# A GRU with a routed FFN on one core: norms of dispatched tokens from SBUF by products with ones, and the chunk work two steps sooner

## The chip, the core and the metric

The kernel runs as one program on one NeuronCore of a Trainium2 chip. The core has five engines that run their own instruction queues in order and meet by semaphores: TensorE (PE, matmuls; PEld is its weight load), VectorE (DVE), ScalarE (ACT), GpSimd (POOL) and SyncE (SP, which here only issues DMAs). The metric is the device time of one execution in microseconds (us); lower is better.

## The reference

A GRU runs over 256 time steps for 16 sequences of width 512. Its outputs are the tokens of a mixture of 8 low-rank experts, and the result is added to x:

```python
def cell(h, x):
    gi = x @ W_ih + b_ih
    gh = h @ W_hh + b_hh
    r = sigmoid(i_r + h_r); z = sigmoid(i_z + h_z)
    n = tanh(i_n + r * h_n)
    h_new = (1 - z) * n + z * h
# for every token h of the 16 x 256:
norm = maximum(linalg.norm(h), 1e-12)
routing = softmax(h / norm @ router_w)          # 8 experts
rw, experts = top_k(routing, 2); rw /= sum(rw)
out = x + sum over the two experts of rw[e] * (h @ Wa[e] @ Wb[e])   # Wa 512x128, Wb 128x512
```

All is float32. Each step of the GRU needs the one before, so the steps form a recurrence; the FFN of finished tokens can run beside it.

## The kernel before

**The recurrence.** `step` issues one GRU step. The state h lies transposed in `hist` (128 partitions: 4 groups of 32 columns; free: 8 steps of a block x 4 quarters q x 48). PE multiplies it with W_hh into PSUM banks `rn` (r and the hidden part of n, L914) and `z` (L924). ACT takes tanh for r (L940), z (L945) and n (L949), DVE does the arithmetic in between (n: L947, L948; zh: L952; m: L954; rows: L956) and transposes the new state back into `hist` (L959). The next step's first matmul waits for that transpose. `back` (L967) makes a row form of h. The input gates x W_ih (`gate_in`, L281 and L289) are done for two steps at a time, half in each step, behind z; for 12 pairs (`EARLY`) they are computed long before and only copied in (`seed`, L261, on ACT).

**Blocks, chunks, slabs.** 8 steps of 16 sequences make a block of 128 tokens. Of 32 blocks the first 29 are *dispatched* and the last 3 are *dense* (`Moe`: all 8 experts). The dispatched blocks form 4 chunks of 7, 11, 7 and 4 blocks (`CHUNKS`). For each block a `Route` keeps its rows in HBM (`keep`: 8 DMAs to H), computes the router's logits (`logits`, L353), the norm, a softmax (`soft1`) and the top two (`soft2`). When a chunk is complete, `Chunk` ranks its tokens by expert (`ranks`, `places`), loads the rows from H again (`fetch`, L545) and scatters them into slots in HBM sorted by expert, by two indirect DMAs per block on POOL (L551). Then each `Slab` (128 slots, one expert) is loaded (L652), gets its expert's weights by two POOL copies (L670, L674), is transposed on DVE (L680), goes through two pairs of PE pieces (`down` L691, `up` L706) with ACT copies between (L698, L714), and is stored to HBM. `Combine` gathers each token's two results by indirect DMAs on POOL (L743), adds them with their weights to x on DVE (L757) and stores the output.

**What sets the order.** All these are agents with a list of `Piece`s. In each step `choose` picks pieces whose gap (steps since the agent's last piece) has passed and whose rooms (buffers) are free. Routes and chunks go first; slabs have a due time `by`, and their rate is the work left over the steps left. `advance(0, ...)` issues the pieces' PE work behind the step's gates, `advance(1, ...)` their other work behind `back`. The order so made is then fixed on every engine. `LAG` sets when slabs start: `ready` is a chunk's end + LAG + its blocks. After step 256 the loop goes on with what is left: the end of the slabs, the combines and the dense blocks.

**The Route of a block before.** Steps from the block's end: +1 `keep`; +2 `logits`, then `fetch` (L605: SP reloads the block's 128 rows from H into `ht`) and `soft0` (DVE transposes the logits, L615); +4 `norm` (L620: ACT squares `ht` with a sum along the row; L622: POOL takes the root); +5 `soft1`; +6 `soft2`. The chunk's `ranks` come 7 steps behind the chunk's end. The dense blocks do without a reload: POOL squares h from SBUF (`prep`, L780 and L785), and 16 products with a column of ones (L796) put the sums beside the logits in `rt`.

Of the kernel before, what the change touches and what calls it, by code (L numbers as in the profile page):

```python
# [8 lines left out]
FP = mybir.dt.float32  # L9
# [7 lines left out]
AF = mybir.ActivationFunctionType  # L17
ALU = mybir.AluOpType
# [3 lines left out]
P = 128  # L22
TS = 8
CHUNKS = [7, 11, 7, 4]
LAG = 10

EARLY = list(range(82, 128, 4))

# [16 lines left out]
def gru_moe_kernel(  # L45
# [47 lines left out]
    pe, dve, act, pool, sp = nc.tensor, nc.vector, nc.scalar, nc.gpsimd, nc.sync  # L93
    B, T, D = x.shape
    E, _, R = wa.shape
    NJ = D // P
    NQ = P // 32
# [18 lines left out]
    moe = ctx.enter_context(tc.tile_pool(name="moe", bufs=2))  # L116
# [29 lines left out]
    for side, src in enumerate((b_ih, b_hh)):  # L146
        for g in (0, 2, 1):
            tag = ("xg", "wbg")[side]
# [34 lines left out]
    ones = const.tile([P, 1], FP, name="ones")  # L183
    pool.memset(ones, 1.0)
    half = const.tile([P, 1], FP, name="half")
# [37 lines left out]
    rt = ps_r.tile([P, 512], FP, name="rt")  # L223
    pe.matmul(rt, lhsT=zero[:, 0:P], rhs=zero, start=True, stop=True)
    banks = []
    for n in range(2):
        pair = []
        for what in ("rn", "z"):
            g = ps_g.tile([P, 512], FP, name=f"{what}_{n}")
            for j in range(NJ):  # L230
                pe.matmul(
                    g[32 * j : 32 * j + 32, :], lhsT=zero[:, 0:32], rhs=zero,
                    start=True, stop=True,
# [5 lines left out]
    for n, parts in enumerate((((0, 0), (1, 0)), ((1, 2),), ((0, 2),), ((0, 1), (1, 1)))):  # L239
        for k, (side, g) in enumerate(parts):  # L240
            for j in range(NJ):
                pe.matmul(
                    bias_ps[32 * j : 32 * j + 32, n * P : (n + 1) * P],
                    lhsT=ones_sq[0:1, 0:32],
                    rhs=b_rows[side, g][:, j * P : (j + 1) * P],
                    start=(k == 0), stop=(k == len(parts) - 1),
# [97 lines left out]
    def tokens(h, q, c):  # L344

        b0 = 16 + 4 * c
        return h[:, :, q, b0 : b0 + 4].rearrange("p t b -> p b t")

    def router(h):

        for q in range(NQ):
            for c in range(NJ):
                pe.matmul(  # L353
                    rt[32 * c : 32 * c + E, 0:32].rearrange("p (b t) -> p b t", t=TS),
                    lhsT=wr_sb[:, q, :], rhs=tokens(h, q, c),
                    start=(q == 0), stop=(q == NQ - 1),
                )

    class Early:
# [55 lines left out]
        def plan(self):  # L415
            pieces = [
                Piece(then=[("load",)], takes="early"),
                Piece(gap=2, then=[("turn",)], takes="at"),
            ] + [
                Piece(gap=0, cost=c, pe=[("into", what, q)])  # L420
                for what, c in (("rn", 0.43), ("z", 0.22))
                for q in range(NQ)
            ] + [Piece(then=[("store",)], gives="early")]
            pieces[2].gap, pieces[2].takes = 1, ["ps"]
            pieces[9].then, pieces[9].gives = [("keep",)], ["ps", "at"]
            return pieces


    class Chunk:
# [113 lines left out]
        def fetch(self, k):  # L543
            ht = moe.tile([P, D], FP, tag="ht2", bufs=2, name=f"ht2_{self.c}_{k}")
            sp.dma_start(ht, self.rows[k].rearrange("b t d -> (b t) d"))  # L545
            self.ht = getattr(self, "ht", {})
            self.ht[k] = ht
# [21 lines left out]
        def plan(self):  # L569
            k = self.k  # L570
            pieces = [
                Piece(gap=7, cost=0.9, pe=[("ranks",)],
                      then=[("places",), ("places2",)]),
                Piece(then=[("places3",)]),
                Piece(then=[("experts",)]),
                Piece(then=[("weights",)]),
            ] + [Piece() for _ in range(k - 2)]
            pieces[0].then[:0] = [("fetch", m) for m in range(2)]
            for m in range(k):
                pieces[2 + m].then.append(("scatter", m))  # L580
                if m + 2 < k:
                    pieces[2 + m].then.append(("fetch", m + 2))
            return pieces

    class Route:
# [14 lines left out]
                    )  # L600
            self.chunk.rows.append(hd)

        def fetch(self):
            self.ht = moe.tile([P, D], FP, tag="ht", name=f"ht_{self.i}")
            sp.dma_start(  # L605
                self.ht, self.chunk.rows[self.k].rearrange("b t d -> (b t) d")
            )

        def logits(self):
            router(self.hist)  # L610

        def soft0(self):

            self.lg = moe.tile([P, 32], FP, tag="lgs", name=f"lg_{self.i}")
            dve.transpose(self.lg, rt[:, 0:32])  # L615

        def norm(self):
            i = self.i
            ss = moe.tile([P, 1], FP, tag="ss", name=f"ss_{i}")
            act.activation(self.ht, self.ht, AF.Square, accum_out=ss)  # L620
            self.nrm = moe.tile([P, 1], FP, tag="nrm", name=f"nrm_{i}")
            pool.tensor_tensor(self.nrm, ss, half, ALU.pow)  # L622

        def soft1(self):
            self.ex, self.sm = softmax(self.i, self.lg, self.nrm)
# [5 lines left out]

        def plan(self):
            return [
                Piece(then=[("keep",)]),
                Piece(cost=0.35, pe=[("logits",)], then=[("fetch",), ("soft0",)]),
                Piece(gap=2, then=[("norm",)]),
                Piece(then=[("soft1",)]),
                Piece(then=[("soft2",)]),
            ]
# [362 lines left out]
    ends = [TS * sum(CHUNKS[: c + 1]) for c in range(len(CHUNKS))]  # L1002
    ready = [e + LAG + k for e, k in zip(ends, CHUNKS)]
    n_slabs = [(2 * P * k + (P - 1) * E) // P for k in CHUNKS]
# [101 lines left out]
    for i in range(NB):  # L1106
        rows, rows_next = rows_next, None
        for t in range(TS):
# [8 lines left out]
            elif m + 1 < T // 2:  # L1117
                q = 0 if t % 2 == 0 else 2
# [72 lines left out]
```

## Time and profile before

| | |
|---|---|
| median of 17 runs | 1366.45 us (1364.02 to 1370.59) |
| profiled execution, device time | 1366.55 us |
| its span, first to last instruction | 1364.8 us |
| mean granted TensorE clock | 0.991 |
| last transpose of the state (L959) ends | 1282.4 us |
| DMA traffic | 158.67 MB |

Instructions in the profile are named by line, engine, operation and tiles (out<-in), with their shapes. A float32 matmul has two records. Lines of the timeline begin with the start and the duration in us; equal instructions in a row are merged (x32); brackets name the idle time before and what ended it. In groups, the numbers behind the bar are busy us, mean ns of one, and idle time before. "issue" is time in which an engine waited for nothing that the profile shows. Two L959 lines in a row bound one step of the GRU.

### The profile page before, as it was taken

To read this page: it belongs to the slowest core of one execution; us is meant where nothing else is said; L and a number is where in the kernel's file an instruction comes from. 1 tells how busy PE (TensorE), PEld (TensorE's weight loads), DVE (VectorE), ACT (ScalarE), POOL (GpSimd) and SP (SyncE) were. 2 spreads that over 40 slices of the span, in tenths; PEclk is the share of its full clock that TensorE was granted. 3 is DMA by queue.
4 is the path that set the end of the run, shared out by engine and by line. 5 is a ranking of instruction groups with operands and counts; after the bars stand their busy time and mean duration, and the time that the engine had idled before them with its cause. 6 is when DMAs were issued, how large, how long until landed. Compare 5 with 4: busy or idle time off the path is not lost. (4 is left out here: it accounts for less than half of the span.)

```text
span 1364.8 us, 68450 instructions
## 1 busy us (share of the span) xinstructions
PE 1291.5 (95%) x30378; PEld 934.2 (68%) x30378; DVE 734.3 (54%) x2678; ACT 392.4 (29%) x1354; POOL 284.5 (21%) x504
## 2 busy tenths in 40 slices
PE   6799999999999999999999899999998999989996
PEld 2477777776677777777776567877766787768752
DVE  1445555555555555555556456566565556656543
ACT  1222222222233333333232233333332332323220
POOL 2000000002221000000002413221124033353452
PEclk7999999999999999999999999999999999999998
DMA  8522322223322111111123534553335245564685
GB/s 196 155 87 89 129 91 78 87 66 114 103 77 67 57 58 41 57 57 57 43 73 111 179 99 138 155 152 112 98 127 184 89 143 163 170 201 135 190 258 170
DMA packets 149477, 158.67 MB, mean 116 GB/s; under 512 B 22646, under 2 KB 103606, under 8 KB 149180
## 3 DMA queue, kind: packets, MB, share of 16 engines
q1 hardware_dynamic: 139760, 123.83, 30.6%
q0 software_dynamic: 9280, 30.42, 7.0%
q8 instruction: 238, 3.90, 1.2%
q14 instruction: 59, 0.48, 0.1%
q10 hardware_dynamic: 140, 0.05, 0.0%
HBM read 84.21 MB, written 69.99 MB: 113 GB/s over the span
## 5 line engine op out<-in xcount | busy, mean ns | idle before, releaser
L914 PE MATMUL rn<-whh,hist 128*32 128x256 f32 x8160 | 505.3, 382 | 24.7 <-DVE hist L959 17.7
L914 PEld LDWEIGHTS rn<-whh,hist 128*32 128x32 f32 x8160 | 266.3, 110 | 198.7 <-DVE hist L959 52.9
L281 PE MATMUL rn<-wih,xT 128*32 128x256 f32 x3712 | 306.6, 382 | 12.5 <-DMA wih<-in_L_cond_W_ih_dram 7.7
L924 PE MATMUL z<-whh,hist 128*32 128x128 f32 x8160 | 288.8, 273 | 7.9 <-issue 7.6
L947 DVE SCALAR_TENSOR_TENSOR n<-r,rn 128x128 f32<-128x128 f32 x256 | 73.4, 287 | 398.7 <-ACT r L940 388.5
L924 PEld LDWEIGHTS z<-whh,hist 128*32 128x32 f32 x8160 | 246.3, 110 | 52.9 <-issue 15.5
L289 PE MATMUL z<-wih,xT 128*32 128x128 f32 x3712 | 206.0, 274 | 5.0 <-ACT z L945 3.1
L940 ACT ACTIVATE r<-rn 128x128 f32<-128x128 f32 x256 | 70.9, 277 | 462.3 <-PE rn L914 439.4
L289 PEld LDWEIGHTS z<-wih,xT 128*32 128x32 f32 x3712 | 137.5, 111 | 77.5 <-issue 6.7
L281 PEld LDWEIGHTS rn<-wih,xT 128*32 128x32 f32 x3712 | 126.9, 111 | 22.8 <-issue 15.8
L952 DVE SCALAR_TENSOR_TENSOR zh<-z,h 128x128 f32<-128x128 f32 x255 | 77.2, 303 | 87.5 <-ACT z L945 86.8
L945 ACT ACTIVATE z<-z 128x128 f32<-128x128 f32 x256 | 71.0, 277 | 172.6 <-PE z L924 148.0
L691 PE MATMUL at_ps<-xgT,wag 128*32 128x128 f32 x2752 | 109.4, 273 | 5.3 <-issue 4.5
L622 POOL TENSOR_TENSOR nrm<-ss,half 128x1 f32<-128x1 f32 x29 | 16.2, 558 | 443.6 <-ACT ht L620 416.3
L706 PE MATMUL y_ps<-wbg,at 128*32 128x256 f32 x1376 | 102.8, 380 | 1.7 <-ACT at L698 0.8
L691 PEld LDWEIGHTS at_ps<-xgT,wag 128*32 128x32 f32 x2752 | 87.7, 110 | 14.7 <-issue 10.9
L959 DVE STREAM_TRANSPOSE hist<-rows 128x128 f32<-128x128 f32 x256 | 79.8, 312 | 8.7
L967 DVE STREAM_TRANSPOSE h<-hist 128x128 f32<-128x128 f32 x256 | 79.7, 311 | 8.7
L674 POOL COPY wbg<-wb_sb 128x512 f32 x86 | 55.9, 650 | 125.6 <-PE y_ps L706 125.6
L956 DVE SCALAR_TENSOR_TENSOR rows<-zh,m 128x128 f32<-128x128 f32 x256 | 75.9, 296 | 8.9
L949 ACT ACTIVATE n<-n 128x128 f32<-128x128 f32 x256 | 77.4, 303 | 8.8 <-DVE n L948 8.0
L954 DVE SCALAR_TENSOR_TENSOR m<-z,n 128x128 f32<-128x128 f32 x256 | 77.7, 304 | 2.6 <-ACT n L949 1.5
(136 smaller groups left out, 1042.8 us busy)
## 6 DMA issues: line engine op xcount, KB each, us to landing
xg<-x_slots SPq DMA_DIRECT2D x344, 64.0 KB
y_slots<-y SPq DMA_DIRECT2D x86, 256.0 KB
ht<-H SPq DMA_DIRECT2D x58, 256.0 KB
x_slots<-zero SPq DMA_DIRECT2D x50, 256.0 KB
x<-in_x_dram SPq DMA_DIRECT2D x256, 32.0 KB
xr<-in_x_dram SPq DMA_DIRECT2D x32, 256.0 KB
out_dram<-xr SPq DMA_DIRECT2D x32, 256.0 KB
H<-rows SPq DMA_DIRECT2D x232, 32.0 KB
```

Source lines behind the costliest of these rows:

```text
L281: pe.matmul(rn[32 * j : 32 * j + 32, 0 : 3 * P].rearrange("p (g d) -> p g d", g=3)[:, 0:3:2, :], lhsT=xts[m][:, q, :], rhs=w[:, 0:3:2, j, ...
L289: ins = pe.matmul(zb[32 * j : 32 * j + 32, 0:P], lhsT=xts[m][:, q, :], rhs=w[:, 1, j, :], start=False, stop=(q == NQ - 1), skip_group_chec ...
L691: pe.matmul(self.ps[c32, 0:P], lhsT=self.wa[:, q, c32], rhs=self.xt[:, q, :], start=(q == 0), stop=(q == NQ - 1),)
L706: pe.matmul(self.ps[c32, half], lhsT=self.at[:, c32], rhs=self.wb[:, half], start=True, stop=True,)
L914: pe.matmul(rn[32 * j : 32 * j + 32, 0 : 2 * P].rearrange("p (g d) -> p g d", g=2), lhsT=hT[:, q, :], rhs=w(q, j)[:, 0:3:2, :], start=Fals ...
L924: pe.matmul(zb[32 * j : 32 * j + 32, 0:P], lhsT=hT[:, q, :], rhs=w(q, j)[:, 1, :], start=False, stop=(q == NQ - 1), skip_group_check=True,)
L949: act.activation(n, n, AF.Tanh)
L952: dve.scalar_tensor_tensor(zh, z, 1.0, hrow, ALU.add, ALU.mult)
L954: dve.scalar_tensor_tensor(m, z, 1.0, n, ALU.subtract, ALU.mult)
L956: dve.scalar_tensor_tensor(hn, zh, 0.5, m, ALU.mult, ALU.subtract)
L959: dve.transpose(hist[:, t, :, lo : lo + 32], hn.rearrange("p (q c) -> p q c", q=NQ))
L967: dve.transpose(hrow.rearrange("p (q c) -> p q c", q=NQ), hT)
```

## The change

The Route no longer reloads its rows. With `keep`, ACT squares the four quarters of h from `hist` into `sq`, and two POOL adds sum the quarters. Behind the logits, four products with a column of ones put the sums of squares into columns 32 to 63 of `rt`; `soft0` transposes both at once, and POOL takes the root from there. `fetch` and `norm` are gone, so `soft1` and `soft2` come two steps sooner, at +3 and +4. `LAG` is 8 instead of 10, and the ranks come 5 steps behind the chunk's end instead of 7; with them scatters, slabs and combines are planned two steps sooner. The planner's cost of the logits piece is 0.4 instead of 0.35.

```diff
-LAG = 10
+LAG = 8
...
-                Piece(gap=7, cost=0.9, pe=[("ranks",)],
+                Piece(gap=LAG - 3, cost=0.9, pe=[("ranks",)],
                       then=[("places",), ("places2",)]),
...
-        def fetch(self):
-            self.ht = moe.tile([P, D], FP, tag="ht", name=f"ht_{self.i}")
-            sp.dma_start(
-                self.ht, self.chunk.rows[self.k].rearrange("b t d -> (b t) d")
-            )
+        def square(self):
+            i = self.i
+            sq = moe.tile([P, NQ, P], FP, tag="ht", name=f"sq_{i}")
+            for q in range(NQ):
+                act.activation(
+                    sq[:, q, :].rearrange("p (b t) -> p b t", t=TS),
+                    self.hist[:, :, q, 16:32].rearrange("p t b -> p b t"),
+                    AF.Square,
+                )
+            pool.tensor_add(sq[:, 0:2, :], sq[:, 0:2, :], sq[:, 2:4, :])
+            pool.tensor_add(sq[:, 0, :], sq[:, 0, :], sq[:, 1, :])
+            self.sq = sq

         def logits(self):
             router(self.hist)
+            for c in range(NJ):
+                pe.matmul(
+                    rt[32 * c : 32 * c + 1, 32:64],
+                    lhsT=ones, rhs=self.sq[:, 0, 32 * c : 32 * c + 32],
+                    start=True, stop=True,
+                )

         def soft0(self):
-            self.lg = moe.tile([P, 32], FP, tag="lgs", name=f"lg_{self.i}")
-            dve.transpose(self.lg, rt[:, 0:32])
-
-        def norm(self):
             i = self.i
-            ss = moe.tile([P, 1], FP, tag="ss", name=f"ss_{i}")
-            act.activation(self.ht, self.ht, AF.Square, accum_out=ss)
+            lg = moe.tile([P, 2, 32], FP, tag="lgs", name=f"lg_{i}")
+            dve.transpose(lg.rearrange("p n e -> p (n e)"), rt[:, 0:64])
+            self.lg = lg[:, 0, :]
             self.nrm = moe.tile([P, 1], FP, tag="nrm", name=f"nrm_{i}")
-            pool.tensor_tensor(self.nrm, ss, half, ALU.pow)
+            pool.tensor_tensor(self.nrm, lg[:, 1, 0:1], half, ALU.pow)
...
-                Piece(then=[("keep",)]),
-                Piece(cost=0.35, pe=[("logits",)], then=[("fetch",), ("soft0",)]),
-                Piece(gap=2, then=[("norm",)]),
+                Piece(then=[("keep",), ("square",)]),
+                Piece(cost=0.4, pe=[("logits",)], then=[("soft0",)]),
                 Piece(then=[("soft1",)]),
                 Piece(then=[("soft2",)]),
```

## The prediction

> **What bounds the kernel now.** I read the page first, then single steps in the timeline, then the groups by line, the chain, and stretches of the tail.
>
> ```profile
> PE 1291.5 (95%) x30378; PEld 934.2 (68%) x30378; DVE 734.3 (54%) x2678; ACT 392.4 (29%) x1354; POOL 284.5 (21%) x504
> ...
> ht<-H SPq DMA_DIRECT2D x58, 256.0 KB
> ```
>
> TensorE is busy nearly throughout; half of the 58 reloads of H (the routes' 29) go. A quiet step with logits, from the timeline:
>
> ```profile
> 483.06 0.31 DVE L959 STREAM_TRANSPOSE hist<-rows 128x128 f32<-128x128 f32 x1
> 483.43 1.93 PE L914 MATMUL rn<-whh,hist 128*32 128x256 f32 x32
> 485.18 1.06 PE L924 MATMUL z<-whh,hist 128*32 128x128 f32 x32
> 486.05 0.62 PE L281 MATMUL rn<-wih,xT 128*32 128x256 f32 x8
> 487.35 0.64 PE L353 MATMUL rt<-hist,wr_sb 128*8 128x32 f32 x32
> 487.46 0.31 DVE L959 STREAM_TRANSPOSE hist<-rows 128x128 f32<-128x128 f32 x1
> 487.83 1.93 PE L914 MATMUL rn<-whh,hist 128*32 128x256 f32 x32
> ```
>
> From hist to hist is 4.40 us, the length of the recurrence through PE, ACT and DVE, and quiet steps keep to it. PE's own work in a step is 1.75 us for rn (483.43 to 485.18), 0.87 for z, 1.31 for the input gates (486.05 to 487.35): 3.93. So 0.47 us of other PE work is free, the logits (0.41 from L353's start to where rn could start) fill that, and anything over it lengthens the step. A slab's piece takes 0.43. A step is thus the larger of 4.405 and 3.93 plus its pieces (2.61 where the gates came early).
>
> Summed over steps 8 to 255 in the program's order this gives 1130 us; the trace has 1205. The 75 us more lie where POOL issues indirect DMAs. One pair and PE behind it:
>
> ```profile
> 1126.12 1.08 POOL L743 DMA_INDIRECT yg<-y_slots,ihi  x1 [0.17 <-issue]
> 1127.43 0.38 PE L289 MATMUL z<-wih,xT 128*32 128x128 f32 x3
> 1127.51 1.00 POOL L743 DMA_INDIRECT yg<-y_slots,ilo  x1 [0.30 <-issue]
> 1128.18 0.44 PE L289 MATMUL z<-wih,xT 128*32 128x128 f32 x5 [0.38 <-issue]
> 1128.94 0.67 PE L281 MATMUL rn<-wih,xT 128*32 128x256 f32 x8 [0.32 <-issue]
> ```
>
> PE gets a few matmuls out every 0.75 us, waiting for nothing that the profile names. 48 pairs (29 scatters, 19 gathers) run before step 256 ends: at most 1.5 us a pair. The change removes none of them.
>
> The end is set by DMAs, in the chain that ended last:
>
> ```profile
> 1347.33 5.47 DMA out_dram<-xr
> ...
> 1352.81 4.47 DMA xr<-in_x_dram
> ...
> 1358.01 1.42 DVE xr L757 x2
> ```
>
> PE ends at 1354.35, but the last dense block's sum (L873) has its x only at 1357.3: that load waits for a buffer that block 26's store to HBM holds.
>
> **The change part by part.** The sum is made against the profiled execution, 1364.8 us of span and 1.75 around it, 1366.55; the median of the runs is 0.1 lower.
>
> Prices from the groups by line:
>
> ```profile
> L796 PE MATMUL rt<-sq,ones 128*1 128x32 f32 x96 | 1.6, 193 | 0.0
> L620 ACT ACTIVATE ht<-ht 128x512 f32<-128x512 f32 x29 | 18.0, 621 | 0.0
> L403 POOL TENSOR_TENSOR ge<-ge,bias 128x256 f32<-128x256 f32 x12 | 8.8, 730 | 0.0
> ```
>
> (a) *Products with ones*: 4 matmuls a block, 8 records, 1.6 us x 8/96 = 0.13 us. In the quiet step above the logits end just as hist does, so 0.03 is hidden at most: 29 x 0.10 to 0.13 gives 2.9 to 3.9. I take **+3.2** (14 logits steps stand alone in the new order at 0.09, 15 beside slab work at 0.13).
>
> (b) *Squares*: 4 ACT instructions on 128x128. A tanh of that size is 277 ns (L945), so 1.1 us; POOL's copy with the same strided operand is 466 ns (L780) against 290 for a plain one (L401), so 1.8 at most. They stand behind the step's last tanh (482.37 in a quiet step) and the next ACT instruction on the recurrence is r at 485.43: 3.0 us of cover, less 0.58 for a slab's y copy and 0.27 for its mid copy. **0**; beyond cover only with an early-gate copy too (0.65), about 0.3 in a few steps.
>
> (c) *Two POOL adds*, 0.73 (L403) and 0.46 us (L402). They can start when the squares are done, about hist time, and end 1.3 us later; PE's logits come 4.3 us after that hist. New: PE, and with it the whole recurrence, waits for POOL there, and DVE's transpose of the logits behind it. Ahead of the adds on POOL stand scatters and gathers. Their starts against their planned steps: all 29 scatters ran 3 to 12 us early, the gathers 8 us early to 3.8 us late (K7 and K9 alone over 0.5 late). Bounds 0 and 29 x 1.3 = 38; nearest row: POOL idle most of the time, **+0.3**.
>
> (d) *Norm on ACT, reload and its wait on SP* go: 29 x (0.62 + 0.19) us of ACT that was under the same cover, and 29 of SP's issues (0.34 to 0.37 us each, in order behind the 8 writes of H). No wait of ACT for this reload is in the waits view, and the quiet reload step is 4.40. Yet five steps with a norm are 12.4 us over their sum (3.4, 3.6, 1.2, 1.9, 2.4). They also hold seven indirect pairs, 9.1 us at 1.3. What is left, 3.3, is the most that goes; **-0.3**. The nrm by POOL stays at 0.57 (L808), and soft1 still comes one step behind it.
>
> (e) *Two steps sooner*: ranks, scatters, slabs and gathers all move, with their SP loads and POOL copies, past the same recurrence. In the built program's order 42 slab pieces stand behind the last step instead of 48: 2.6 us less there, 2.6 more before, since steps near the end are over 4.405 already. The sum over steps rises by 7.6 in all; 3.2 are (a), 2.6 these pieces. The other **+1.8** are pieces that fall together in steps without cover while others keep idle PE time. One gather pair moves from the tail, where 0.43-us groups of 512-wide matmuls partly hide the stall, to a step: **+0.6** (0 to 1.5). The tail is PE's (68.4 us busy of the 72.0 up to 1354.4), so it gives the **2.6** back (net 0 with the above).
>
> (f) *The end*: in the new order DVE does block 26's last sum before the last dense block's second scale (L838), not behind it. Then its store starts about 1344.9 instead of 1347.3, and x for L873 is there at about 1354.9, half a microsecond behind PE. Behind L873 only one add stands (0.75) instead of three. From PE's end to the span's end is 10.4 us now; then 0.5 + 0.7 + 0.75 + 4.6 (last add to end, 1360.2 to 1364.8) = 6.5. Bounds -1 (only the order of adds helps) and -4.5; I take **-3.5**.
>
> (g) *A rule weighed against (c)*: two lines of the timeline at 650 us.
>
> ```profile
> 650.66 0.70 POOL L674 COPY wbg<-wb_sb 128x512 f32 x1
> 650.80 0.70 DVE L954 SCALAR_TENSOR_TENSOR m<-z,n 128x128 f32<-128x128 f32 x1
> ```
>
> This m takes 0.70 us where an undisturbed one takes 0.28, beside a POOL copy. 28 of the 768 instructions of zh, m and rows (L952, L954, L956) are stretched, by 8.4 us in all, about half of them in steps where POOL had been held by soft2's mask and its copies then fell on the recurrence. The Trainium skill (SBUF — State Buffer, Who interferes with whom) says that a VectorE instruction with two SBUF inputs and a GpSimd instruction that reads SBUF exclude each other, whoever starts first; the new adds read SBUF, so by the rule alone each of 29 pairs could stretch the recurrence by some 0.4 us, 12 us in all. By the rows they do not meet: rows ends 0.65 us behind the tanh (482.37 to 483.02), four squares need at least 0.7 at the spacing of two tanhs (0.17), and zh follows 3.5 us later.
>
> Sum: 3.2 + 0.3 - 0.3 + 1.8 + 0.6 - 3.5 = +2.1, so 1368.65 for such an execution, **1368.6** against the median: 0.15% slower, inside the 0.2% (2.7 us) that a measurement of this kernel can tell from no change.
>
> **The rivals.**
>
> *Slower, the adds meet the recurrence*: POOL comes to them late, behind gathers or copies, and either PE waits or zh and m are stretched. Against: POOL's lead above; for: it is half busy in stretches (8.0 of 16 us from 764 to 780). 11 blocks beside slabs and combines x 0.4 to 0.7 us: +4 to +8, 1373 to 1377. It decides if the adds start later than hist + 1.5 us.
>
> *Slower, no gain at the end*: x of the last dense block is late all the same, since stores and loads at the end share the DMA engines. Term (f) becomes -1: 1371.
>
> *Faster, the reload's traffic stretches the stalls*: then steps with a norm, and the pairs near them, get back what (d) leaves out: -3.3 more, and 29 x 0.25 MB of 158.7 MB, 4.8% of the 75 us, another -3.6. Together 2.1 - 6.6 = -4.5: 1362. For: the norm steps' lengths; against: step 64 has four indirects, no norm, and is 4.1 over. It decides if stalls a pair fall below 1.3 us.
>
> *Not what it says*: without effect if the tail were not PE's; 68.4 of 72.0 us speak against.
>
> **How the numbers follow.** Forecast 0.48 (with (a), (e) and (f) at their ends, 1366.5 to 1371.5: 0.31 inside the bound, 0.17 above); adds 0.18 and no gain at the end 0.12, both slower, two in twelve of the latter inside; faster 0.22, of it 0.20 below the bound. So faster 0.20, within 0.2% 0.35, slower 0.45. The range, 1362 to 1375, leaves out a tenth on either side.
>
> **What would show it.** Right: logits steps 4.50 instead of 4.40; no PE wait named POOL at the products; about 0.75 us of stall per indirect DMA as before; last hist some 8 us later and span end 6 us nearer to it; the end 6 to 7 us behind PE. Wrong: DVE's zh, m, rows above 0.30 on the mean, PE waits on POOL's adds, or quiet steps that move at all.

## The result, and the profile after

The changed kernel takes 1385.7 us (median; 1378.2 to 1389.1) against 1367.0 for the kernel before beside it: a ratio of 1.0132, 95% interval 1.0118 to 1.0147. It is 1.3% slower, 17 us more than forecast and outside the range.

The head of the page of the changed kernel:

```profile
span 1382.4 us, 68813 instructions
...
PE 1302.6 (94%) x30610; PEld 932.8 (67%) x30610; DVE 743.1 (54%) x2678; ACT 411.4 (30%) x1412; POOL 321.7 (23%) x562
```

The span has grown by 17.6 us, of which PE's busy time accounts for 11. Read by place, the 17.6 us are nearly all ahead of the last step. The last hist stands at 1299.7 us instead of 1282.4 (+17.3), and from there to the end it takes 82.7 us instead of 82.4. The forecast had +8 and -6. The last hist of the changed kernel:

```profile
1299.39 0.31 DVE L970 STREAM_TRANSPOSE hist<-rows 128x128 f32<-128x128 f32 x1
```

The quiet step with logits that the prediction showed, in the timeline of the changed kernel:

```profile
483.35 0.31 DVE L970 STREAM_TRANSPOSE hist<-rows 128x128 f32<-128x128 f32 x1
...
484.02 0.74 POOL L613 TENSOR_TENSOR sq<-sq 128x256 f32<-128x256 f32 x1 [12.68 <-ACT sq L608]
484.84 0.46 POOL L614 TENSOR_TENSOR sq<-sq 128x128 f32<-128x128 f32 x1
...
487.64 0.64 PE L353 MATMUL rt<-hist,wr_sb 128*8 128x32 f32 x32
487.75 0.31 DVE L970 STREAM_TRANSPOSE hist<-rows 128x128 f32<-128x128 f32 x1
488.07 0.26 PE L620 MATMUL rt<-sq,ones 128*1 128x32 f32 x8
...
488.73 0.55 POOL L634 TENSOR_TENSOR nrm<-lg,half 128x1 f32<-128x1 f32 x1 [3.44 <-DVE lg L631]
```

From hist to hist it is 4.40 us still: the eight product records lie under the start of the next step. The adds are over 2.3 us before the logits and 2.8 before the products that need them, about as forecast. What is new is in the brackets. POOL stands 12.7 us until the squares are there, and 3.4 us until DVE has transposed the logits.

POOL's longest waits over the whole run (total us, times, longest), first in the changed kernel:

```profile
POOL sq L613 <- ACT sq L608: 422.7, 29, 71.6
POOL pre L642 <- DVE mask L330: 241.9, 29, 10.0
POOL wbg L685 <- PE y_ps L717: 96.2, 28, 8.3
POOL nrm L634 <- DVE lg L631: 86.3, 29, 4.2
```

and in the kernel before:

```profile
POOL nrm L622 <- ACT ht L620: 416.3, 27, 85.6
POOL pre L630 <- DVE mask L330: 232.8, 28, 10.3
```

Once a block POOL caught up with the recurrence and stood still. Before, this was at the norm, two steps behind the logits. Now it is at the block's last hist, one step ahead of them, and again in the logits step. POOL is idle all the same, so nothing looks dear here; but all indirect DMAs that come behind these two places in POOL's order now start after them.

Where they then start can be counted: of the 97 indirect DMAs between steps 8 and 255 of the kernel before, 8 are issued in a step with logits; of 98 in the changed kernel, 20 (one or two fewer or more, by where a step is taken to end). The sum of the steps by the prediction's rule rises from 1130.4 to 1138.5 us (+8.1; the prediction had 7.6), and what the trace has over that sum rises from 75.1 to 85.7 (+10.6, where the forecast had none beyond the rule); the first eight steps are 1.4 shorter, which gives the 17.3. In the 29 steps with logits alone that excess goes from 5.4 to 16.3 us.

The granted TensorE clock shows a second price. Between 100 us and the end of PE's work it is never halved in the profiled execution of the kernel before. In that of the changed kernel it is halved in three stretches, from 1129.8, 1201.4 and 1331.1 us, 17 us in all. The first of them, the 3.4 us ahead of it, and the product that runs in it (a stretch has its length, PE's busy us with the number of records, the granted clock, and DMA's share and GB/s):

```profile
1126.39:1129.80 3.41, 0.52 (x13) 0.99 0.93 253
1129.80:1133.21 3.41, 3.41 (x45) 0.51 0.49 135
1129.46 3.41 PE L925 MATMUL rn<-whh,hist 128*32 128x256 f32 x32 [2.89 <-DVE hist L970]
```

The product takes 3.41 us, where it takes 1.93 in the quiet step. All 47 such stretches in the profiles of this case come directly behind 3.4 us in which PE was busy for 61% at most (here 15%), be it by one gap or by stalls beside several indirect DMAs. The reverse does not hold: the kernel before has two places where PE is busy for less than half of 3.4 us, and no halved clock behind them. Half of PE's busy time in the three stretches is 7.4 us, an estimate of the most that they cost. These 7.4 us are not beside the excess and the end, but part of them: 4.6 ahead of the last hist and 2.8 behind it.

### The profile page after: what moved, and what is told of

The parts are those of the page before. It is cut to its first block, busy times and chain, and to the rows that moved or that the text cites. A ratio compares the mean times of both kernels' runs of the same rounds, so it can differ in the third digit from the quotient of the medians.

```text
span 1382.4 us, 68813 instructions
## 1 busy us (share of the span) xinstructions
PE 1302.6 (94%) x30610; PEld 932.8 (67%) x30610; DVE 743.1 (54%) x2678; ACT 411.4 (30%) x1412; POOL 321.7 (23%) x562
## 4 chain that ended last, share of the span: by engine, by line
PE 83%; DVE 5%; DMA 4%; issue 3%; another core or an unknown queue 2%; SPq 2%; ACT 1%; DVEq 0%; ACTq 0%
PE rn L925 33%; PE z L935 15%; PE rn L281 13%; PE z L289 6%; PE y_ps L717 5%; PE at_ps L702 4%; PE gi L387 1%; PE a_ps L837 1%; PE rt L353 1%; PE o_ps L874 1%; DMA whh<-in_L_cond_W_hh_dram 1%; DMA wih<-in_L_cond_W_ih_dram 1%; DVE zh L963 1%; DVE rows L967 1%
## 5 line engine op out<-in xcount | busy, mean ns | idle before, releaser
L281 PE MATMUL rn<-wih,xT 128*32 128x256 f32 x3712 | 310.4, 383 | 13.8 <-DMA wih<-in_L_cond_W_ih_dram 7.1
L935 PE MATMUL z<-whh,hist 128*32 128x128 f32 x8160 | 285.2, 273 | 4.3 <-issue 3.9
L613 POOL TENSOR_TENSOR sq<-sq 128x256 f32<-128x256 f32 x29 | 22.1, 763 | 422.7 <-ACT sq L608 422.7
L725 ACT COPY y<-y_ps 128x512 f32<-128x512 f32 x86 | 50.2, 584 | 109.8 <-PE y_ps L717 104.9
L959 DVE SCALAR_TENSOR_TENSOR n<-n,rn 128x128 f32<-128x128 f32 x256 | 73.6, 287 | 8.7
```

The costliest lines, as they stand in the source:

```text
L281: pe.matmul(rn[32 * j : 32 * j + 32, 0 : 3 * P].rearrange("p (g d) -> p g d", g=3)[:, 0:3:2, :], lhsT=xts[m][:, q, :], rhs=w[:, 0:3:2, j, ...
L935: pe.matmul(zb[32 * j : 32 * j + 32, 0:P], lhsT=hT[:, q, :], rhs=w(q, j)[:, 1, :], start=False, stop=(q == NQ - 1), skip_group_check=True,)
L959: dve.scalar_tensor_tensor(n, n, 0.5, rn[:, 2 * P : 3 * P], ALU.mult, ALU.add)
```

## The experiments

The kernels of one group ran one after the other on one chip, with the kernel before. The groups ran on different chips, and one chip turned out to be another case altogether (third group). Ratios are to the kernel before on the same chip.

### First group: the parts one at a time

**norm10**, the norms alone (LAG also sets the ranks' gap, which is 7 again):

```
-LAG = 8
+LAG = 10
```

> The new norms alone (squares on ACT, two adds on POOL, products with ones, no reload), with the ranks, slabs and gathers at their old steps. Theory S (the shift by two steps is the loss): 1364 to 1369 us, last hist within 3 us of before's 1282.4, since the quiet steps with logits of the changed kernel were 4.40 us long as before, so the products cost nothing. Theory N (the norms are the loss, through POOL, whose norm now waits for DVE's transpose and holds up the scatters and gathers queued behind it): 1378 to 1386 us, last hist at 1292 or later, with the excess over the sum of the steps near scatters and gathers grown as in the changed kernel (85.7 against 75.1 us).

Measured: 1378.0 us against 1368.9, ratio 1.0083 (1.0050 to 1.0117). Last hist at 1291.0, excess 80.6 us, from last hist to the end 81.8. Theory N holds, though with half of the loss (its last hist was to be at 1292 or later): the norms cost 9 us by themselves, all of it ahead of the last step. 21 indirect DMAs are in steps with logits.

Step 226 of this run shows it best. It has the same pieces as in the kernel before, where it took 5.66 us and held no indirect DMA; here it takes 7.51. POOL and PE, from its timeline:

```profile
1115.90 1.19 POOL L613 TENSOR_TENSOR sq<-sq 128x256 f32<-128x256 f32 x1 [13.60 <-ACT sq L608]
1117.17 0.47 POOL L614 TENSOR_TENSOR sq<-sq 128x128 f32<-128x128 f32 x1
1117.85 0.61 POOL L681 COPY wag<-wa_sb 128x512 f32 x1 [0.21 <-issue]
1118.40 0.61 POOL L685 COPY wbg<-wb_sb 128x512 f32 x1
1119.17 1.04 POOL L754 DMA_INDIRECT yg<-y_slots,ihi  x1 [0.15 <-issue]
...
1119.99 0.31 PE L353 MATMUL rt<-hist,wr_sb 128*8 128x32 f32 x6
1120.36 0.37 PE L353 MATMUL rt<-hist,wr_sb 128*8 128x32 f32 x3
1120.52 1.00 POOL L754 DMA_INDIRECT yg<-y_slots,ilo  x1 [0.30 <-issue]
1121.48 0.31 PE L353 MATMUL rt<-hist,wr_sb 128*8 128x32 f32 x4 [0.75 <-issue]
1122.24 0.47 PE L353 MATMUL rt<-hist,wr_sb 128*8 128x32 f32 x18 [0.45 <-issue]
```

Held until the block's hist at 1115.5, POOL does the adds, then two copies, then the gather pair that in the kernel before had run in step 224 (its first half at 1103.81). PE gets a few matmuls out at a time, with pauses of up to 0.75 us, as it did with the larger ones in the lines of the prediction. Here they are the logits' short ones, and the 32 records that take 0.64 us in a quiet step are spread over 2.7 (1119.99 to 1122.71). The step that the pair left got shorter (224: 6.70 to 5.20 us), so the move costs 0.35 us net here; the loss is a sum of many such moves, not one long wait.

**slab8**, the old norms, with slabs and combines two steps sooner and the ranks where they were (gap 7 is a constant in the kernel before):

```
-LAG = 10
+LAG = 8
```

> The old norms with their reload; slabs and gathers two steps sooner, the ranks and scatters at their old steps. Theory S: slower, 1374 to 1384 us, because the sum over the steps grows by 4.8 us (1135.2 against 1130.4, worked out from the order), gathers fall on steps without cover, and the tail's order of SP is close to that of the changed kernel. Theory N: 1364 to 1370 us.

Measured: 1379.7 us, ratio 1.0086 (1.0060 to 1.0112). Theory S holds too: each theory named half of the loss. At the last hist the halves are 8.6 and 13.1 us and the change has 17.3, so they overlap. Last hist is at 1295.5 (+13.1): the sum of the steps is up by 4.8 as worked out, the excess by 10.1 (85.2). Only 7 indirect DMAs are in steps with logits, but the steps that hold the 98 are 0.83 us over the sum for each, where it was 0.73 for the 97 of before. From last hist to the end it takes 82.8 us, not the 75 that fewer pieces and a shorter end would give. Its profile has five halved stretches of the clock, 8.2 us at most by the estimate above, 6.6 of it ahead of the last hist; so a good part of the excess may be the clock. DVE stands 7.75 us in block 29's last sum, for its x.

**rank5**, the new norms with only the ranks and scatters sooner:

```
-LAG = 8
+LAG = 10
...
-                Piece(gap=LAG - 3, cost=0.9, pe=[("ranks",)],
+                Piece(gap=5, cost=0.9, pe=[("ranks",)],
```

> The new norms; ranks, places and scatters two steps sooner, slabs and gathers at their old steps. If the scatters' new place is the loss (chunk 3's four scatters among the gathers of K11 to K13: steps 237 to 240 took 13.7 us over their sum in the changed kernel): 1371 to 1380 us, most of it gained between steps 236 and 243. If the slabs' and gathers' new place is the loss: 1364 to 1369 us. Theory N: 1378 us or more.

Measured: 1382.6 us, ratio 1.0108 (1.0082 to 1.0134), last hist at 1299.3. The interval overlaps that of norm10, so the ranks' place is not resolved. Steps 236 to 242 lose 3.8 us to the kernel before, less than a third of the loss, and step 243 gives 2.2 of it back. Most of the loss is that of the norms, as theory N had it.

**own_after**, the dense blocks' x in a buffer of its own:

```
-            self.xr = moe.tile([P, D], FP, tag="xr", bufs=3, name=f"xr_{i}")
+            self.xr = moe.tile([P, D], FP, tag="ht", name=f"xr_{i}")
```

> The changed kernel with the dense blocks' x in the buffers that the squares used, so that this load no longer waits on SP for a combine's store; the order of every engine is the same. Theory T (the loss behind the last step is SP's queue held by that load): PE's wait of 3.8 us for a slab's turn near 1332 us goes, the 8.4 us wait of DVE for x of block 29 goes, and the time falls by 4 to 8 us, 1378 to 1382. Rival: PE is held there by the indirect DMAs and the bank count all the same; 1384 to 1387.

Measured: 1382.4 us, ratio 1.0095 (1.0062 to 1.0128), 82.1 us from last hist to the end. Theory T falls, though the time lies between its range and the rival's. The load no longer waits (1326.83, 24.3 us behind last hist instead of 27.8), but it is still planned one step ahead of the sum. The sum starts at 1334.39, DVE has stood 8.4 us in it as before, and PE waits 4.15 us for the same turn.

### Second group: undoing single parts

**dve10**: norm10 with the adds on DVE, and the norm's power on POOL two steps later, where it was.

```
-            pool.tensor_add(sq[:, 0:2, :], sq[:, 0:2, :], sq[:, 2:4, :])
-            pool.tensor_add(sq[:, 0, :], sq[:, 0, :], sq[:, 1, :])
+            dve.tensor_add(sq[:, 0:2, :], sq[:, 0:2, :], sq[:, 2:4, :])
+            dve.tensor_add(sq[:, 0, :], sq[:, 0, :], sq[:, 1, :])
...
+        def norm(self):
+            self.nrm = moe.tile([P, 1], FP, tag="nrm", name=f"nrm_{self.i}")
+            pool.tensor_tensor(self.nrm, self.ss, half, ALU.pow)
...
+                Piece(gap=2, then=[("norm",)]),
```

> The new norms at the old steps as in the run before, but the two adds on DVE and the norm's power on POOL two steps behind the logits again, where it was: POOL's order is then that of the kernel before, with one wait in the same place. Theory P (of the norms' 9 us most is POOL, held at the two new waits, so that indirect DMAs start in steps with logits: 21 of 97 there against 8): 1369 to 1373 us, about 8 indirect DMAs in steps with logits, last hist at 1283 to 1286. Rival R (the products on PE are the cost, or the ACT squares): 1376 to 1381 us, and indirect DMAs in logits steps fall without a gain.

Measured: 1363.7 us against 1363.9, ratio 0.9998 (0.9980 to 1.0017). Theory P holds, and all of the loss goes where it had most of it. With squares, products and no reload, but without the two new waits of POOL, the 9 us are gone. 13 indirect DMAs are in steps with logits, where about 8 were expected. POOL's waits in this run:

```profile
POOL pre L644 <- DVE mask L330: 361.8, 29, 18.5
POOL nrm L636 <- DVE lg L631: 230.5, 19, 77.1
```

The wait for the squares is gone, and the norm's comes two steps behind the logits again, in 19 of 29 blocks.

**prod**, the products alone, on the kernel before:

```
         def logits(self):
             router(self.hist)
+            for c in range(NJ):
+                pe.matmul(
+                    rt[32 * c : 32 * c + 1, 32:64],
+                    lhsT=ones, rhs=zero[:, 32 * c : 32 * c + 32],
+                    start=True, stop=True,
+                )
```

> The kernel before with four more products with ones in each logits step, on a tile of zeros whose result nobody reads: the products' price on PE by itself. The prediction had 3.2 us for them (1369 to 1371). By the quiet steps of the changed kernel, 4.40 us as before, they are hidden there and cost 0.13 us only in the 15 logits steps beside slab work: 0 to 2 us, 1367 to 1370. Rival R: 1374 or more.

Measured: ratio 1.0020 (1.0002 to 1.0037), 0.3 to 5 us, in the middle 2.7. The price forecast, 3.2, lies inside. Since dve10 is level, squares for reload may give back about as much as the products cost; with intervals of some 2.5 us to either side, this is not shown.

**early8**, the changed kernel with the dense x loaded some five steps sooner, in buffers of its own (tag as in own_after):

```
-            pieces[14].then, pieces[14].takes = [("load",)], ["xr"]
-            pieces[19].then, pieces[19].gives = [("store",)], "ps aT xr".split()
+            pieces[6].then = [("load",)]
+            pieces[19].then, pieces[19].gives = [("store",)], "ps aT".split()
```

> The changed kernel with the dense blocks' x in buffers of their own and its load some five steps sooner (at the fifth piece of the down products instead of at the third of the up products). Theory D (behind the last step DVE stands 8.4 us in a dense block's last sum, whose x was loaded one step ahead, and the slab turns queued behind it on DVE hold PE for 3.8 us): DVE's waits of 8.4 us for x of blocks 29 and 30 go, PE has no gap over 1 us there, and from last hist to the end it takes 72 to 78 us instead of 82.7; 1376 to 1381 us. Rival (the end is bound by the gathers' and stores' traffic): 81 to 84 us from last hist to the end, 1383 to 1388.

Measured: 1376.9 us, ratio 1.0080 (1.0052 to 1.0109): 5 parts in a thousand under the changed kernel's ratio. From last hist to the end it takes 79.9 us instead of 82.7. What was to go is gone. DVE and PE in the tail of the changed kernel, by waits:

```profile
DVE xr L884 <- DMA xr<-in_x_dram: 8.4, 1, 8.4
```

```profile
PE at_ps L702 <- DVE xgT L691: 3.8, 1, 3.8
```

and DVE in that of early8:

```profile
DVE xr L884 <- PE o_ps L874: 7.8, 2, 6.4
```

There the last sums wait for PE alone, and PE waits for no turn any more (the longest wait left for it is 1.1 us of issue).

Theory D is right on the wait; the 79.9 us lie between its range and the rival's.

**early_before**, the same edit on the kernel before.

> The same edit on the kernel before, where DVE waits about 5 us for x of block 29 and the last dense block's x comes 3 us behind PE's end. Theory D: 3 to 7 us faster than before, 1360 to 1364 us, all of it behind the last step. Rival: 1365 to 1369.

Measured: ratio 0.9988 (0.9972 to 1.0005), not told from no change. So no price of this wait is shown in the order of the kernel before.

### Third group: a chip without the stalls

**late10**: norm10 with the norm's power two steps later as in dve10, and the adds left on POOL. **slab12**: the kernel before with LAG = 12. **plain_before**: every indirect DMA of the kernel before replaced,

```
-            for ix in self.idx:
-                ins = pool.indirect_dma_start(
...
+            for s in (2 * k, 2 * k + 1):
+                ins = sp.dma_start(
+                    self.x[s * P : (s + 1) * P, :], self.ht[k][:, :]
+                ).ins
...
-                pool.indirect_dma_start(
...
+                s = 2 * self.k + n
+                sp.dma_start(y[:, :], ch.y[s * P : (s + 1) * P, :])
```

and **plain_slab8**: the same with LAG = 8.

> The new norms at the old steps, adds on POOL as in the change, but the norm's power on POOL two steps behind the logits as before: of the two new waits of POOL only the adds' is left (for the squares, at the hist that ends a block). If the power's wait for DVE's transpose in the logits step is the 9 us: 1362 to 1367 us. If the adds' wait is: 1371 to 1377. Half each: 1367 to 1371.

> The old norms, slabs and gathers two steps later than before (ranks and scatters unmoved). If the steps' place decides by chance of what falls together (phase): slower or faster by up to 10 us without a rule, within 1358 to 1375. If sooner is worse because more slab work and one more gather pair stand ahead of the last step beside stalls: faster in the scan by 3 to 8 us and 2 to 3 us longer behind it, 1358 to 1364 us.

> The kernel before with every indirect DMA (scatters and gathers, 116 in all) replaced by a plain DMA of the same 256 KB on SP, to and from fixed rows; the routing of rows is left out. If the 75 us over the sum of the steps are PE's stalls beside POOL's indirect DMAs: last hist at 1207 to 1220 us instead of 1282.4, about 1285 to 1300 us in all. Rival (the traffic of the rows itself, or DVE's places and weights, lengthen these steps): last hist at 1250 or later, 1330 us or more.

> The same with slabs and combines two steps sooner. If the 10.7 us that this shift cost with indirect DMAs are stalls that fall on steps without idle PE time: within 4 us of the run beside it (the packing alone gives 4.8 us more in the scan and 2.6 less behind it). If the loss is elsewhere (slab loads on SP, DVE's turns, the tail): 8 to 13 us above the run beside it.

Measured, against a kernel before that takes 1308.3 us on this chip, 55 to 60 us less than on the others: late10 0.9979 (0.9964 to 0.9995), slab12 1.0046 (1.0030 to 1.0062), plain_before 1.0046 (1.0032 to 1.0060), plain_slab8 1.0158 (1.0141 to 1.0175).

None of these expectations can be read as meant, because what they were to take away is not there. The trace of late10 has the logits step that was shown above, with the same gather pair in it:

```profile
1066.62 1.04 POOL L757 DMA_INDIRECT yg<-y_slots,ihi  x1 [0.15 <-issue]
...
1067.60 0.64 PE L353 MATMUL rt<-hist,wr_sb 128*8 128x32 f32 x32
...
1067.96 1.00 POOL L757 DMA_INDIRECT yg<-y_slots,ilo  x1 [0.30 <-issue]
1068.04 0.51 PE L620 MATMUL rt<-sq,ones 128*1 128x32 f32 x8
```

POOL is busy as long as before (1.04 and 1.00 us), but PE gets the logits out in 0.64 us. The excess over the sum of the steps is 11.9 us in the whole run, about 0.1 per indirect DMA. With no stall left to remove, plain_before gains nothing. Its transfers now queue on SP, and its excess is 26.5 us; 13.1 of them are a single wait of PE behind ACT, which stands 15.4 us for a reload of H that comes behind scatters on SP.

Two things can still be taken from the group. slab12 is slower, with last hist at 1222.2 (late10: 1221.1), but 89.0 us from there to the end: the slabs two steps later do not pay either. And plain_slab8 is 15 us above plain_before by the medians, 11.3 in the profiled executions, 8.2 of these ahead of the last hist. So without an indirect DMA the shift still costs: 4.8 us of packing, and behind the last step a wait of PE of 7.3 us for a slab's turn on DVE. The rest was not taken apart.

### Fourth group: the two waits once more, on a chip with stalls

**late10_again**, **norm10_again** and **after_again** are the kernels of those names; **early_dve10** is dve10 with the edit of early8.

> The adds' wait on POOL alone, together with the kernel that has both waits, on one chip. On a chip where an indirect DMA stalls PE by some 0.75 us: if the power's wait in the logits step is the norms' loss, 0.2% under before to level with it (ratio 0.998 to 1.002); if the adds' wait is, 1.005 to 1.009. On a chip where the stall is 0.1 us: 0.997 to 1.000, as in the run above.

> Both waits. On a chip with stalls of 0.75 us 1.006 to 1.010, as measured. On a chip with stalls of 0.1 us: if the loss is made of stalls that POOL's order puts into worse steps, 0.997 to 1.002; if it is POOL's waits by themselves (copies on the recurrence, PE waiting), 1.005 to 1.010 there too.

> The changed kernel once more beside them. On a chip with stalls of 0.75 us 1.011 to 1.015, as measured. On a chip with stalls of 0.1 us: if all its loss is stalls, 0.995 to 1.003 (the sum of the steps 4.8 us up, the end 3.5 to 6 us down); if the shift by two steps costs without stalls too, as the plain DMAs' 15 us suggest, 1.006 to 1.012.

> The candidate for a better kernel: the new norms with the adds on DVE and the power two steps later, old steps, and the dense blocks' x sooner into buffers of their own. From the two parts (0.9998 and 0.9988): 0.997 to 1.000, 1 to 4 us faster than before; the reloads of 29 blocks are gone. Rival: the parts undo each other, 1.000 to 1.003.

Measured, against 1367.9: late10_again 1373.9, ratio 1.0045 (1.0023 to 1.0067); norm10_again 1.0069 (1.0048 to 1.0090); after_again 1.0121 (1.0082 to 1.0159); early_dve10 0.9993 (0.9976 to 1.0011). In steps with logits there are 18, 21, 20 and 13 indirect DMAs.

The adds' wait is worth about 5 us (late10_again against early_dve10, intervals apart, though early_dve10 also has the earlier x). The power's wait adds about 3, and here the intervals overlap, so its share is not settled. By kinds of steps, norm10_again has 11 us more over the sum in the logits steps than early_dve10, 7 more in the steps of soft2, and 14 less in all others; the profiled runs differ by 6.4 us at the last hist. More telling is late10 on two chips: the same kernel is 0.2% faster than before where an indirect DMA costs about 0.1 us, and 0.45% slower where it costs 0.74. That points to the stalls as what the adds' wait costs, but the granted clock moves with it. On the chip with stalls its mean is 0.985 in the runs of late10_again, against 0.991 before and 0.991 in early_dve10; on the other chip it is 0.990 against 0.988 before. The profile of late10_again has four halved stretches ahead of the last hist, 6.6 us at most by the estimate above; that of late10 has none there. How the 6 us divide between the stalls themselves and the halved clock behind them was not separated. norm10 and the changed kernel did not run on the chip without stalls; how much of theirs would be left there stays open.

early_dve10 is level with the kernel before. No run gave a version that is faster than before by more than a measurement can tell on a chip with stalls.

### Fifth group: the adds undone in the changed kernel

**dve8** is the changed kernel with the two adds on DVE, **early_dve8** the same with the edit of early8.

> The changed kernel with only the two adds moved from POOL to DVE; the power stays in the logits step, as two steps sooner need it. From the runs at the old steps (both waits 1.007 to 1.008, the power's alone not run, none 0.9998) the adds' wait is worth 3 to 7 us: 1379 to 1383 us on a chip where before takes 1367, ratio 1.008 to 1.011, and fewer than 20 indirect DMAs in steps with logits. If the two-step shift holds them there all the same: 1.012 to 1.014.

> The same with the dense blocks' x sooner in buffers of their own, which gave the changed kernel some 5 us (1.008 against 1.013): if the parts add up, ratio 1.002 to 1.006; what is left is then the shift by two steps and the power's wait. If they don't: 1.007 or more. Not faster than before in either case by the sum.

Measured, against 1362.9: dve8 1.0108 (1.0070 to 1.0146), early_dve8 1.0061 (1.0040 to 1.0083). The adds' move is worth a few us, not resolved by itself (18 indirect DMAs stay in steps with logits, held by the power's wait, which two steps sooner make necessary: soft1 comes in the step behind the logits). The two repairs together take away about half of the loss; the ratio is at the upper end of what adding the parts gave. early_dve8 needs 76.8 us from last hist to the end; that is 5.6 less than the 82.4 before, and about the 6 that the prediction expected of the tail.

## Why the prediction was wrong

The sum's terms, one by one, in the profiled execution (predicted +2.1, found 1384.2 - 1366.55 = +17.6):

- **(a) Products, +3.2.** About right in size (2.7, interval 0.3 to 5), wrong in place: up to step 57 all steps keep to 4.40 us, so nothing is paid in quiet steps.
- **(b) Squares, 0.** Right: ACT's busy time grew by 19 us and the adds start 0.4 us behind hist in the quiet step.
- **(c) Adds on POOL, +0.3.** This is the step that failed. "New: PE, and with it the whole recurrence, waits for POOL there": no such wait is in the profile. The question was asked in one direction only, who waits for the adds, with "POOL idle most of the time" as the answer. The adds wait for the squares, and so does the queue behind them: scatters, gathers and copies that had run ahead of the recurrence now start behind a block's hist and behind the logits. By the runs the two waits cost some 8 to 9 us by the medians (norm10_again against early_dve10, norm10 against before), and without them the loss of the norms is gone (dve10).
- **(d) Norm and reload gone, -0.3.** Not settled: dve10 is level although the products cost some 2.7, which would put this term near its bound of -3.3, but the intervals of both runs are as wide as that.
- **(e) Two steps sooner, +1.8, +0.6 and a net 0.** The packing came as worked out (the sum rose by 8.1 where 7.6 was forecast). The price of an indirect DMA was taken as fixed. It depends on where it falls: 0.73 us on the mean before, 0.83 in slab8, 0.81 in the changed kernel, 98 of them. That is nearly 8 us, and up to 4.6 of it is the halved clock behind stalls that fall close together, a cost that the sum did not have at all.
- **The tail, net 0 with the pieces, and (f), -3.5.** The end itself came: from PE's end to the span's end 5.6 us instead of 10.4, -4.8 where -3.5 was taken. But PE did not give the 2.6 us back: from last hist to PE's end it takes 77.1 us, not 69.4. DVE comes to block 29's last sum 22.8 us behind the last hist instead of 25.6, and the load of its x is issued at 27.8 instead of 24.5. So DVE waits 8.4 us there instead of 4.0, and a slab's turn behind it on DVE holds PE for 3.8. slab8 has the same wait with the old norms, and early8 takes it away.
- **(g) The two ports.** The rows were nearer than the rule, though not right. zh, m and rows stretched by over 60 ns: 28 instructions and 8.3 us before, 35 and 10.3 us after, +2.0 us where the rule alone gave 12 and the rows 0. The adds are not the partners. In step 196 of norm10 it is the copies, let go by soft2's wait:

```profile
964.99 0.20 POOL L642 TENSOR_TENSOR pre<-pre,mask 128x8 f32<-128x8 f32 x1 [9.32 <-DVE mask L330]
...
966.77 0.67 POOL L681 COPY wag<-wa_sb 128x512 f32 x1
966.90 0.69 DVE L965 SCALAR_TENSOR_TENSOR m<-z,n 128x128 f32<-128x128 f32 x1
```

The Trainium skill (SBUF — State Buffer, Who interferes with whom) names the pair of operations rightly: beside the copy, m takes 0.69 us instead of 0.28. How often they meet is, in lines like these, set by what POOL last waited for.

Of the rivals, "the adds meet the recurrence" had the right engine, and its 1373 to 1377 us are close to what norm10 takes (1377 and 1378); but it had POOL come late to the adds, and POOL stood waiting for them: in all 29 blocks they start 0.3 to 0.4 us behind hist. "What would show it" was right on PE's waits and nearly so on the distance from PE's end (5.6 us, forecast 6 to 7); its lines on the last hist (8 us later, found 17) and on the end (6 us nearer to it, found 0.3 further) show the two places where it failed.

## What to carry to other kernels

When an instruction with a wait is moved in the order of an engine that issues DMAs, list what stands behind it in that order and when it will now start; an idle engine is not a free place for a wait. A transfer's issue that disturbs another engine has a price that depends on what that engine has to issue at the moment, so count, for each kind of step, how many fall into it before and after, and look at the granted clock behind places where several come close together. When work behind the last step gets shorter, look which load was planned just one step ahead of its use.

## What the runs showed of the hardware

The kernel before takes 1363 to 1369 us on four of the chips and 1308 on a fifth. The traces of the latter have PE's stalls of 0.75 us beside POOL's indirect DMAs nearly gone (excess 11.9 us in late10 there, 77.0 in the same kernel on a chip with stalls), with POOL's own time for them unchanged. What makes the chips differ was not found; the granted clock does not (0.988 on the mean for the kernel before on the fifth, 0.990 to 0.991 on the others). On a chip with stalls, 32 logits records of 0.64 us in all took 2.7 us beside one gather pair, so short instructions are not spared; no run varied their size by itself.

The halved clock goes with the stalls. On the chips with stalls its stretches cost, by the estimate above, at most 1.7 us in the profiles of before, prod, early_before, dve10 and early_dve10, which are near the time of the kernel before, and at most 1.3 to 8.5 us in those of the slower ones.
